# A batch's first scatter alone waits, earlier first loads and table fill, and three late jobs in a set order, in a two-layer cross-attention and mixture-of-experts kernel

## The chip, the cores and the metric

The kernel runs on one core of a Trainium2 chip. The metric is the time of one launch on the device in microseconds (us), as the median of several runs. Of the core's engines, PE (TensorE) multiplies matrices, and its weight loads are shown apart as PEld; DVE (VectorE) does element-wise work and reductions; ACT (ScalarE) does activations and copies; POOL (GpSimd) does some element-wise work and issues indirect DMAs; SP (SyncE) issues most of the loads. ACT and POOL issue DMAs of their own too.

## What is computed

`x` has 8 batches of 512 rows of 256 numbers; `ctx` has 64 rows of 256 for each batch. All is float32.

```
x = x + xattn0(layernorm(x), ctx)      # 16 heads of 16, softmax over 64 keys
x = x + ffn0(layernorm(x))             # per batch, the 384 rows with the highest router score
                                       # become gelu(row @ w_block), the others pass through
x = x + xattn1(layernorm(x), ctx, mask)
x = x + moe(layernorm(x))              # 8 experts, top 2 per row, softmax weights over the two
    moe: for each expert e: weight_e * (silu(row @ gate_e) * (row @ up_e)) @ down_e,  inner size 1024
```

## The kernel before

**Front part.** x lies in SBUF as 32 tiles of 128 rows. Each batch goes through one chain of 62 steps (L1183): attention of layer 0, the routed feed-forward, attention of layer 1, and the routing for the experts. A normalisation is `stats` (L373: batch statistics on DVE, then rstd by a power on POOL, L384), `scaled` (L387: a shift on DVE, then four ACT instructions, L393) and two `turned` steps (L401: transposes on PE into ps_x, copied by ACT). In the attentions `by_tokens` (L451) makes scores whose maxima DVE takes (L477), `by_keys` (L489) makes them again, turned, for ACT's exponentials (ex, L510), and `values`, `divided` and `added` finish. `biased` (L427) adds an output bias to x on POOL. Scores and exponentials share one PSUM buffer. Other chains are the constants ("s", `setups`, sorted by a number given to each), keys and values of the context ("k", "v"), ranks of the router ("A" to "H"), the lists of jobs ("l") and seven early expert jobs ("j").

The string `ORDER` (L49) says which chain takes its next step; 0 to 7 are the batches. `in_order` (L1209) ties each step's instructions on PE, DVE, ACT and POOL behind those of the steps ahead of it on the same engine, without a semaphore. So ORDER is the order of each engine's queue in the front part; loads on SP are not tied by it.

**First loads** (L157 to L192). SP starts with the context (ctxT, two halves), ACT with wk of layer 0, the four tiles of batch 0 and bk; POOL with wv, bv and bq of layer 0; SP goes on with wv and bv of layer 1, then wq, bo, wo of layer 0, batch 1 and all later things. vbd (L307) is a table that has to be filled with zeros once, half by DVE and half by POOL, before context values are put in; its fill has the number -0.85 among the constants, behind bq's scaling and ahead of headm.

**Scatter** (`sent_off`, L804). At the end of its chain each batch writes every row, with its number and weights, to two places in a DRAM buffer `xs` that is sorted by expert: two indirect DMAs from POOL for each of four row tiles, eight in all. They are declared free of each other, but the eighth takes a wait on the seven others, so that it can stand for all of them in what waits for the batch: the first early load waits for batch 3's last (L1083), and later batches follow it. Only the last batch's eight are waited for one by one.

**Late part.** 36 expert jobs of 256 rows ("full"), 128 rows ("one") or twice 64 rows ("pair"), in a fixed `order` (L1422): full, full, then pair, full, and one or full in turn. For each, `load` (L1251) reads expert and row numbers from the lists on SP and loads rows (xg) and 3 MB of weights, 6 MB for a pair; `enter` (L1305) turns the rows into xjT; `gate_up_full` or `gate_up_rows` multiplies by gate and up; `turn` (L1383) transposes the result of small jobs; `down` (L1391) multiplies by the down weights and adds the weighted rows to the output by an indirect DMA (L103). A pair's rows also wait for scatters of zero rows that pad the lists (L1029 to L1036). Only the first job's gates and the entries of the first two jobs are tied by `in_order`; for the rest of the late part the order on each engine is chosen when the program is built. The loop (L1437) enters the next job, then multiplies the job before it down.

Of the kernel before, what the change touches and what calls it, by code (L numbers as in the profile page):

```python
# [16 lines left out]
B = 8  # L17
# [7 lines left out]
TB = S // P  # L25
# [3 lines left out]
TOPK = 2  # L29
# [9 lines left out]
NLATE = NFULL - NEARLY  # L39
NONE = 7  # L40
NPAIR = 11
NJOB = NLATE + NONE + NPAIR
NUNIT = 2 * NPAIR
BIG = 65536.0
NG = H // 2
QR = 32
NQ = P // QR

ORDER = """  # L49
sssss0sss0ksk0s1020001s0k110s1vs0s031010s7s2s40v320v2410030v20120ss01040502A010A30A0As10  # L50
1013010343201130005s12010sk0112151761Bs2B1BB112120241201v102s2050223s022302412C22123C2C0
21C02131012110323150030sv02411033123104102523105200004331323426D14D34Ds14D2341v233613421
63233344212345412615434311432513431414312E25124E544E452356E54722434237252346535264345645
256352452F362F2325F63F464556355473355463574536743566474353567335566346v37l64763G464jj77j
5jGj666j5j7jj47Gjjj765j7457j4G5j64654j7j6556747j5j76446444j4746sH6jj56j557j76j7j57jj7Hsj
76jjjjHH7565j65jj676jj7jj6j57j5j6j75557j555jj57j6j667j7jjjs67j66j76j7676j66j76s667j676jj
jj7jjj77j7j7jjjjj77jjs7j7j7j7j7j77jj7jjjljj7jj7jj
"""


# [1 line left out]
def xattn_ffn_kernel(ctx: ExitStack, tc: tile.TileContext, a: dict, out: bass.AP):  # L62
    nc = tc.nc
# [25 lines left out]
    def after(i, others):  # L89
        for other in others:  # L90
            tc.add_manual_dep(
                i, other.name,
                mybir.DependencyInfo(mybir.DependencyClass.Sync, mybir.DependencyReason.DATA),
                reason="rows that it needs",
            )

    def apart(i, others, reason):
        for other in others:
            tc.declare_no_dep(i, other, reason=reason)
# [14 lines left out]
    with ExitStack() as front:  # L114
# [36 lines left out]
        def load_layer(l, names, q):  # L151
            for n in names:
                how = load_mat if n[0] == "w" else load_col if n in ("bk", "bq") else load_row
                layers[l][n] = how(q, f"{n}{l}")
# [6 lines left out]
            )  # L161
        load_layer(0, ("wk",), nc.scalar)
        for t in range(TB):
            nc.scalar.dma_start(x_sb[:, t, :], x_t[0][:, t, :])
        load_layer(0, ("bk",), nc.scalar)
        load_layer(0, ("wv", "bv", "bq"), nc.gpsimd)
        load_layer(1, ("wv", "bv"), nc.sync)
        load_layer(0, ("wq", "bo", "wo"), nc.sync)
        nc.sync.dma_start(x_sb[:, TB : 2 * TB, :], x_t[1])
        load_layer(1, ("wk", "bk"), nc.sync)  # L170
# [128 lines left out]
        turn = [0]  # L299
# [8 lines left out]
        for l in range(2):  # L308
            layers[l]["vbd"] = vbd[:, l]
        setups.append((  # L310
            -0.85, lambda: (nc.vector.memset(vbd[:, 0], 0.0), nc.gpsimd.memset(vbd[:, 1], 0.0)),
        ))

        def keys(l, c):
# [378 lines left out]
        def route_steps(b):  # L693
# [110 lines left out]
            def sent_off(t):  # L804
                slots, xr = got["slots"], got["xn"]

                sent = scattered.setdefault(b, [])
                for k in range(TOPK):  # L810
                    i = nc.gpsimd.indirect_dma_start(  # L811
                        out=xs,
                        out_offset=bass.IndirectOffsetOnAxis(ap=slots[:, t, k : k + 1], axis=0),
                        in_=xr[:, t, :],
                        in_offset=None,
                    ).ins
                    final = len(sent) == TB * TOPK - 1 and b < B - 1
                    if b >= B // 2:
                        apart(i, early_loads, "rows of other batches")
                    for other_i in sent:  # L820
                        if final:
                            tc.add_manual_dep(
                                i, other_i.name,
                                mybir.DependencyInfo(
                                    mybir.DependencyClass.Sync, mybir.DependencyReason.DATA
                                ),
                                reason="the last scatter stands for all",
                            )
                        else:
                            tc.declare_no_dep(i, other_i, reason="rows of their own")  # L830
                    sent.append(i)
                routed[:] = sent[-1:] if b < B - 1 else sent

            steps += [gates, logits, chosen, counted, weighed, placed]
            return steps + [lambda t=t: sent_off(t) for t in range(TB)]
# [227 lines left out]
        def early_steps(j):  # L1063
            got = {}

            def load():
                if not e_w:
                    e_w["gu"] = wpool[0].tile([P, NC, 2 * FF], F32, tag="wgu", name="e_wgu")
                    e_w["dn"] = wpool[0].tile([P, NF, D], F32, tag="wdn", name="e_wdn")
                with tc.issue_after(last.pop().ins) if last else nullcontext():  # L1070
                    row = nc.sync.value_load(
                        jobs_early[0:1, 0, j : j + 1], min_val=0, max_val=E * QROWS - P
                    )
                    e = nc.sync.value_load(jobs_early[0:1, 1, j : j + 1], min_val=0, max_val=E - 1)
                i = nc.sync.dma_start(
                    e_xg, xs[bass.ds(row, 2 * P), :].rearrange("(s p) w -> p s w", p=P)
                ).ins
                early_loads.append(i)

                for b in scattered:  # L1080
                    if b >= B // 2:
                        apart(i, scattered[b], "rows of other batches")
                after(i, scattered[B // 2 - 1][-1:])  # L1083
                got["e"] = e

            def load_piece(n):
# [122 lines left out]
        def in_order(step):  # L1209
            traced = nc.cur_bb.bb.instructions  # L1210
            last = traced[-1].name
            step()
            made = []
            for i in reversed(nc.cur_bb.bb.instructions):
                if i.name == last:
                    break
                made.append(i)
            for i in reversed(made):
                if i.engine not in engines:
                    continue  # L1220
                ahead = behind.setdefault(i.engine, [])
                for other in ahead:
                    tc.add_manual_dep(
                        i, other,
                        mybir.DependencyInfo(
                            mybir.DependencyClass.NoSync, mybir.DependencyReason.DATA
                        ),
                        reason="the order of the steps",
                    )

                if "DMA" not in type(i).__name__:
                    ahead.clear()
                ahead.append(i.name)
# [101 lines left out]
    def gate_up_full(j, xT, w):  # L1335
        wgu = w[0][0]
        hT = moe.tile([P, NF, 2 * P], F32, tag="hT", name=f"hT_{j}")
        for f in range(NF):
            ps = ps_gu.tile([P, 2, 2 * P], F32, tag="gu", name=f"gu_{j}_{f}")
            for half in range(2):  # L1340
                o = half * FF + f * P
                for c in range(NC):
                    nc.tensor.matmul(  # L1343
                        ps[:, half, :],
                        lhsT=wgu[:, c, o : o + P],
                        rhs=xT[:, c].rearrange("p s q -> p (s q)"),
                        start=(c == 0),
                        stop=(c == NC - 1),
                    )
            sg = moe.tile([P, 4 * P], F32, tag="sg", name=f"sg_{j}_{f}")  # L1350
            nc.scalar.activation(sg[:, 0 : 2 * P], ps[:, 0, :], AF.Silu)  # L1351
            nc.vector.tensor_tensor(hT[:, f, :], sg[:, 0 : 2 * P], ps[:, 1, :], ALU.mult)  # L1352
        return hT
# [78 lines left out]
    loads = [load_at(0), load_at(1)]  # L1432
    entered = []
    in_order(lambda: entered.append(enter(order[0], loads[0][0])))
    entered = entered[0]
    pending = None
    for i, j in enumerate(order):  # L1437
        xg, w = loads.pop(0)
        xT, tok, wt = entered
        if i > 0:  # L1440
            loads.append(load_at(i + 2))
        if i == 0:

            took_h = []
            in_order(lambda: took_h.append(gate_up_full(j, xT, w)))
            hT = took_h[0]
        elif j < NLATE:
            hT = gate_up_full(j, xT, w)
        else:
            h, hT = gate_up_rows(j, xT, w)  # L1450
        if i == 0:
            small_list()
            unit_list()
            loads.append(load_at(2))
        if i == 0:
            got_rows = []
            in_order(lambda: got_rows.append(enter(order[1], loads[0][0])))
            entered = got_rows[0]
        elif i + 1 < len(order):
            entered = enter(order[i + 1], loads[0][0])  # L1460
        if pending is not None:
            down(*pending)
        if j >= NLATE:
            turn(j, h, hT)
        pending = (j, hT, w, tok, wt)
    down(*pending)

# [44 lines left out]
```

## Time and profile before

| what | value |
|---|---|
| median of 3 runs | 1194.18 us (1190.78 to 1194.49) |
| the profiled execution | 1195.06 us |
| its span, first to last instruction | 1193.3 us |
| mean granted clock of PE | 0.993 |
| instructions | 21070 |
| DVE / ACT / POOL busy | 577.3 / 375.2 / 285.6 us |
| DMA moved | 209.96 MB, mean 176 GB/s |
| scatters to xs (L811) | 64, 975 ns each on POOL |
| indirect adds to the output (L103) | 65 late and 14 early ones |

In rows of the trace the first number is the start in us from the beginning of the span, the second the time in us; then come engine, line, operation, output<-input, shape, and how many instructions are put together. What stands in brackets is the engine's idle time just ahead of the row, and what ended it. The busy row of the page shows each fortieth of the span (29.8 us) as a digit, in tenths. Ends of matmuls are modelled, so a busy PE is not always at its peak. The front part reaches to about 587 us, the late part from there to the end.

### The profile page before, as it was taken

How to read it: one execution, taken by the hardware profiler on the slowest of the kernel's cores; microseconds unless marked ns; L12 is line 12 of the kernel's file. 1: busy time of each engine (PE TensorE's matmuls, PEld its weight loads, DVE VectorE, ACT ScalarE, POOL GpSimd, SP SyncE). 2: the span in 40 equal slices, each digit the busy share in tenths (PEclk: the TensorE clock that was granted, in tenths of full speed). 3: DMA queues.
4: the chain of work that ended last, by engine and by line, in shares of the span. 5: the costliest groups of instructions: out<-in, count | busy, mean ns of one | idle time of the engine just before them, and what ended most of it. 6: DMA issues, size and time to landing. Idle time of an engine off the chain costs nothing. (4 is left out here: it accounts for less than half of the span.)

```text
span 1193.3 us, 21070 instructions
## 1 busy us (share of the span) xinstructions
PE 1161.0 (97%) x8084; PEld 831.6 (70%) x8084; DVE 577.3 (48%) x1670; ACT 375.2 (31%) x718; POOL 285.6 (24%) x311
## 2 busy tenths in 40 slices
PE   6999999989999999999999999999999999999997
PEld 3655665655567778778877776876778767777676
DVE  6898787888787766655722121222222212222211
ACT  3655654644544342322211111211221112211211
POOL 5330223223330412322411212122121121121221
PEclk9999999999999999999999999999999999999999
DMA  9000001010025444445898689868897888967931
GB/s 265 2 1 2 1 19 38 23 51 33 24 80 170 123 127 131 114 146 151 276 340 285 216 284 307 305 209 313 294 310 256 278 302 308 311 227 270 313 112 18
DMA packets 122884, 209.96 MB, mean 176 GB/s; under 512 B 10912, under 2 KB 108064, under 8 KB 110752
## 3 DMA queue, kind: packets, MB, share of 16 engines
q1 hardware_dynamic: 102720, 185.64, 44.5%
q0 software_dynamic: 14848, 17.99, 7.5%
q10 hardware_dynamic: 5216, 4.98, 1.2%
q8 instruction: 64, 1.05, 0.4%
q14 instruction: 36, 0.29, 0.1%
HBM read 186.80 MB, written 23.73 MB: 176 GB/s over the span
## 5 line engine op out<-in xcount | busy, mean ns | idle before, releaser
L1343 PE MATMUL gu<-xjT,wgu 128*128 128x256 f32 x1152 | 253.8, 381 | 0.7 <-ACT xjT L1314 0.7
L1343 PEld LDWEIGHTS gu<-xjT,wgu 128*128 128x128 f32 x1152 | 218.7, 191 | 31.9 <-issue 1.5
L103 POOL DMA_INDIRECT out_dram<-now,tok x65 | 101.1, 1556 | 487.2 <-DVE now L1408 309.9
L1400 PE MATMUL o<-wdn,hT 128*128 128x256 f32 (+1 forms) x1040 | 193.0, 380 | 0.0
L1400 PEld LDWEIGHTS o<-wdn,hT 128*128 128x128 f32 (+1 forms) x1040 | 153.2, 172 | 29.5 <-issue 1.8
L1352 DVE TENSOR_TENSOR hT<-sg,gu 128x256 f32<-128x256 f32 x144 | 60.6, 421 | 192.9 <-ACT sg L1351 187.6
L1370 PE MATMUL gr<-wgu,xjT 128*64 128x512 f32 (+1 forms) x464 | 127.9, 596 | 0.0
L1351 ACT ACTIVATE sg<-gu 128x256 f32<-128x256 f32 x144 | 55.2, 383 | 204.8 <-PE gu L1343 200.7
L1132 PE MATMUL gu_e<-x_sb,e_wgu 128*128 128x256 f32 x448 | 103.2, 387 | 0.6 <-ACT x_sb L1111 0.6
L1132 PEld LDWEIGHTS gu_e<-x_sb,e_wgu 128*128 128x128 f32 x448 | 85.0, 192 | 15.9 <-issue 2.6
L1408 DVE TENSOR_SCALAR now<-o,wt 128x256 f32<-128x256 f32 x54 | 26.1, 484 | 144.2 <-PE o L1400 144.2
L1370 PEld LDWEIGHTS gr<-wgu,xjT 128*64 128x64 f32 (+1 forms) x464 | 45.0, 149 | 72.8 <-issue 71.0
L384 POOL TENSOR_TENSOR rstd<-ve,mhalf 128x4 f32<-128x4 f32 x32 | 32.8, 1026 | 233.8 <-DVE ve L382 180.7
L811 POOL DMA_INDIRECT xs<-xr,slots x64 | 62.4, 975 | 104.5 <-issue 57.6
L477 DVE TENSOR_REDUCE mx<-sc 128x32 f32<-128x2048 f32 x32 | 73.2, 2288 | 22.2 <-PE sc L470 19.0
L1380 DVE TENSOR_TENSOR h<-sg,gr 128x512 f32<-128x512 f32 x36 | 24.7, 687 | 87.3 <-PE gr L1370 87.3
L440 PE MATMUL ps_q<-xT,w_wq 128*128 128x512 f32 x128 | 63.5, 625 | 0.5 <-ACT xT L411 0.5
L1379 ACT ACTIVATE sg<-gr 128x512 f32<-128x512 f32 x36 | 21.5, 597 | 135.1 <-PE gr L1370 135.1
L571 PE MATMUL py<-w_wo,cT 128*128 128x256 f32 x256 | 60.3, 384 | 0.0
L393 ACT ACTIVATE xn<-x_sb,shift,rstd 128x256 f32<-128x256 f32 x96 | 49.8, 593 | 19.6 <-DVE shift L390 18.3
L571 PEld LDWEIGHTS py<-w_wo,cT 128*128 128x128 f32 x256 | 47.3, 190 | 11.6 <-issue 5.3
L379 DVE BATCH_NORM_STATS2 st<-x_sb 128x6 f32<-128x256 f32 x128 | 51.4, 401 | 6.6 <-DMA x_sb<-in_x_dram 6.4
(288 smaller groups left out, 1457.0 us busy)
## 6 DMA issues: line engine op xcount, KB each, us to landing
wgu<-in_guT_dram SPq DMA_DIRECT2D x94, 1024.0 KB
wdn<-in_dnT_dram SPq DMA_DIRECT2D x47, 1024.0 KB
e_wgu<-in_guT_dram SPq DMA_DIRECT2D x56, 256.0 KB
e_wdn<-in_dnT_dram SPq DMA_DIRECT2D x7, 1024.0 KB
xg<-xs SPq DMA_DIRECT2D x18, 260.0 KB
out_dram<-x_sb ACTq DMA_DIRECT2D x8, 512.0 KB
x_sb<-in_x_dram SPq DMA_DIRECT2D x7, 512.0 KB
x_sb<-xs SPq DMA_DIRECT2D x7, 260.0 KB
```

What stands on the lines that cost most here:

```text
L103: i = nc.gpsimd.indirect_dma_start(out=out_rows, out_offset=bass.IndirectOffsetOnAxis(ap=tok, axis=0), in_=rows, in_offset=None, bounds_ch ...
L379: nc.vector.bn_stats(st, x_sb[:, b * TB + t, :])
L440: nc.tensor.matmul(ps, lhsT=w["wq"][:, k, c * P : (c + 1) * P], rhs=got["xT"][:, k, :], start=(k == 0), stop=(k == NC - 1),)
L477: nc.vector.tensor_reduce(got["mx"].rearrange("p t (r h) -> p r t h", r=NQ)[:, :, :, 2 * c : 2 * c + 2], sc, AX.X, ALU.max,)
L571: nc.tensor.matmul(py[:, s, :], lhsT=cT[:, c, t * P : (t + 1) * P], rhs=w["wo"][:, c, :], start=(c == 0), stop=(c == NC - 1),)
L811: i = nc.gpsimd.indirect_dma_start(out=xs, out_offset=bass.IndirectOffsetOnAxis(ap=slots[:, t, k : k + 1], axis=0), in_=xr[:, t, :], in_of ...
L1132: nc.tensor.matmul(ps[:, half, :], lhsT=e_w["gu"][:, c, o : o + P], rhs=e_xT[:, c].rearrange("p s q -> p (s q)"), start=(c == 0), stop=(c ...
L1343: nc.tensor.matmul(ps[:, half, :], lhsT=wgu[:, c, o : o + P], rhs=xT[:, c].rearrange("p s q -> p (s q)"), start=(c == 0), stop=(c == NC - 1),)
L1351: nc.scalar.activation(sg[:, 0 : 2 * P], ps[:, 0, :], AF.Silu)
L1352: nc.vector.tensor_tensor(hT[:, f, :], sg[:, 0 : 2 * P], ps[:, 1, :], ALU.mult)
L1370: nc.tensor.matmul(ps[rows], lhsT=xT[:, c, 0, rows], rhs=wgu[:, c, o : o + 4 * P], start=(c == 0), stop=(c == NC - 1),)
L1400: nc.tensor.matmul(ps[rows], lhsT=hT[:, f, s * P + rows.start : s * P + rows.stop], rhs=wdn[:, f, :], start=(f == 0), stop=(f == NF - 1),)
```

## The change

- ORDER is written anew, with the same steps.
- The fill of vbd gets the number -0.93 and so comes first of all constants, on DVE and on POOL.
- Of batch 0's four tiles two are now issued by ACT and two by SP; wv and bq of layer 0 go from POOL to ACT, behind the tiles; wv of layer 1 comes behind SP's tiles; bv of both layers goes to POOL.
- In a batch's scatter the first waits for the eight of the batch ahead; the other seven are declared free of both batches' scatters. The eighth waits for nothing more, and whatever waited for it waits for all eight.
- The first three jobs of the late part are put through `in_order` in all their steps: entry, gates, the down product of the job ahead, and turn.

```diff
+NPIN = 3
...
 ORDER = """
-sssss0sss0ksk0s1020001s0k110s1vs0s031010s7s2s40v320v2410030v20120ss01040502A010A30A0As10
...
+ssssss0ss0ksk0120000102sk0s11v25001ss0s3400310s2v14ss10s030s20sv172004010A00102A03A01A01
...
         for t in range(TB):
-            nc.scalar.dma_start(x_sb[:, t, :], x_t[0][:, t, :])
-        load_layer(0, ("bk",), nc.scalar)
-        load_layer(0, ("wv", "bv", "bq"), nc.gpsimd)
-        load_layer(1, ("wv", "bv"), nc.sync)
+            q = (nc.scalar, nc.scalar, nc.sync, nc.sync)[t]
+            q.dma_start(x_sb[:, t, :], x_t[0][:, t, :])
+        load_layer(0, ("bk", "wv", "bq"), nc.scalar)
+        load_layer(1, ("wv",), nc.sync)
+        load_layer(0, ("bv",), nc.gpsimd)
+        load_layer(1, ("bv",), nc.gpsimd)
         load_layer(0, ("wq", "bo", "wo"), nc.sync)
...
         setups.append((
-            -0.85, lambda: (nc.vector.memset(vbd[:, 0], 0.0), nc.gpsimd.memset(vbd[:, 1], 0.0)),
+            -0.93, lambda: (nc.vector.memset(vbd[:, 0], 0.0), nc.gpsimd.memset(vbd[:, 1], 0.0)),
         ))
...
-                    final = len(sent) == TB * TOPK - 1 and b < B - 1
                     if b >= B // 2:
                         apart(i, early_loads, "rows of other batches")
-                    for other_i in sent:
-                        if final:
-                            tc.add_manual_dep(
...
-                        else:
-                            tc.declare_no_dep(i, other_i, reason="rows of their own")
+                    if sent:
+                        apart(i, sent + scattered.get(b - 1, []), "rows of their own")
+                    elif b > 0:
+                        after(i, scattered[b - 1])
                     sent.append(i)
-                routed[:] = sent[-1:] if b < B - 1 else sent
+                routed[:] = sent
...
-                after(i, scattered[B // 2 - 1][-1:])
+                after(i, scattered[B // 2 - 1])
...
+    def placed(i, step):
+
+        if i < NPIN:
+            got = []
+            in_order(lambda: got.append(step()))
+            return got[0]
+        return step()
...
     for i, j in enumerate(order):
...
-        if i == 0:
-
-            took_h = []
-            in_order(lambda: took_h.append(gate_up_full(j, xT, w)))
-            hT = took_h[0]
-        elif j < NLATE:
-            hT = gate_up_full(j, xT, w)
+        if j < NLATE:
+            hT = placed(i, lambda: gate_up_full(j, xT, w))
         else:
-            h, hT = gate_up_rows(j, xT, w)
+            h, hT = placed(i, lambda: gate_up_rows(j, xT, w))
...
-        elif i + 1 < len(order):
-            entered = enter(order[i + 1], loads[0][0])
+        if i + 1 < len(order):
+            entered.append(placed(i, lambda: enter(order[i + 1], loads[0][0])))
         if pending is not None:
-            down(*pending)
+            placed(i, lambda: down(*pending))
         if j >= NLATE:
-            turn(j, h, hT)
+            placed(i, lambda: turn(j, h, hT))
```

More of the change, by code (lines that the diff above doesn't have):

```diff
@@ L49 @@
 ORDER = """
-sssss0sss0ksk0s1020001s0k110s1vs0s031010s7s2s40v320v2410030v20120ss01040502A010A30A0As10
[L51 to L57, printed above, removed]
+ssssss0ss0ksk0120000102sk0s11v25001ss0s3400310s2v14ss10s030s20sv172004010A00102A03A01A01
+010310342015v21031030010v021s1v612k511BB2125B021071251B102120201243042s0123202C102032C12
+13122C6C10s12132v10301203502104s331231s14220032102040303130113D4D746D324461D24v323133143
+2632135345341623461245324114241315114E2s541E4E2534E3244324455372724542323255345236344564
+2556354254F32F22655F42353F663546756355345456646357s473455653765336436373l336457j6jj47467
+5jj746G6j5j4j4jGj4j5j7jj6G7jGj67s6j765j5sj45j74j5j67jj5j47j7465754s76j6j7467446H4567j675
+j7H6jH5Hj56j565jjjj67j7jj766j7j5jj5577j56jj75jjj655j6756j6j77j6sj676j7667j6j6677jj667j66
+7jjj7jj7jj77jjjjj77js7jj77jjj77j77jjj7j7jlj7jjjjj
 """
@@ L816, in sent_off @@
                     ).ins
-                    final = len(sent) == TB * TOPK - 1 and b < B - 1
                     if b >= B // 2:
                         apart(i, early_loads, "rows of other batches")
-                    for other_i in sent:
-                        if final:
-                            tc.add_manual_dep(
[L823 to L828, printed above, removed]
-                        else:
-                            tc.declare_no_dep(i, other_i, reason="rows of their own")
+                    if sent:
+                        apart(i, sent + scattered.get(b - 1, []), "rows of their own")
+                    elif b > 0:
+                        after(i, scattered[b - 1])
                     sent.append(i)
-                routed[:] = sent[-1:] if b < B - 1 else sent
+                routed[:] = sent
             steps += [gates, logits, chosen, counted, weighed, placed]
@@ L1434, in xattn_ffn_kernel @@
     in_order(lambda: entered.append(enter(order[0], loads[0][0])))
-    entered = entered[0]
+    def placed(i, step):
[4 more added lines that the diff above has]
+        return step()
     pending = None
     for i, j in enumerate(order):
-        xg, w = loads.pop(0)
-        xT, tok, wt = entered
+        w = loads.pop(0)[1]
+        xT, tok, wt = entered.pop(0)
         if i > 0:
             loads.append(load_at(i + 2))
-        if i == 0:
-            took_h = []
-            in_order(lambda: took_h.append(gate_up_full(j, xT, w)))
-            hT = took_h[0]
-        elif j < NLATE:
-            hT = gate_up_full(j, xT, w)
+        if j < NLATE:
+            hT = placed(i, lambda: gate_up_full(j, xT, w))
         else:
-            h, hT = gate_up_rows(j, xT, w)
+            h, hT = placed(i, lambda: gate_up_rows(j, xT, w))
         if i == 0:
@@ L1454, in xattn_ffn_kernel @@
             loads.append(load_at(2))
[L1455 to L1458, printed above, removed]
-        elif i + 1 < len(order):
-            entered = enter(order[i + 1], loads[0][0])
+        if i + 1 < len(order):
+            entered.append(placed(i, lambda: enter(order[i + 1], loads[0][0])))
         if pending is not None:
-            down(*pending)
+            placed(i, lambda: down(*pending))
         if j >= NLATE:
-            turn(j, h, hT)
+            placed(i, lambda: turn(j, h, hT))
         pending = (j, hT, w, tok, wt)
```

## The prediction

> **What bounds the kernel now.** I read the page's first two parts, then who kept TensorE (PE) waiting, then stretches, then rows in order of time at the start, around the scatters and at the first late jobs.
>
> ```profile
> PE 1161.0 (97%) x8084; PEld 831.6 (70%) x8084; DVE 577.3 (48%) x1670; ACT 375.2 (31%) x718; POOL 285.6 (24%) x311
> PE   6999999989999999999999999999999999999997
> ```
>
> PE is busy in 1161.0 of 1193.3 us. The change takes no matmul away, so it can win only from the 32.3 us in which PE stands, and from time that PE runs slowly. By 25 us stretches the 32.3 divide thus: 9.1 in the first 25 us, 7.4 behind the last matmul (it ends at 1186.04), 15.8 between 25 and 625 us, and nothing from 625 us to the last matmul. The waits of PE:
>
> ```profile
> PE ps_k L318 <- DMA pre<-in_wk_dram: 5.1, 1, 5.1
> PE st L493 <- ACT ex L510: 4.5, 3, 2.5
> PE ps_x L408 <- ACT xn L393: 3.7, 2, 3.5
> PE ps_x L1312 <- DMA xg<-xs: 2.5, 2, 2.3
> ```
>
> Each line gives total us, times, longest. The third line is the start, the second the scatters of batches 0 and 1, the fourth the first late jobs. PE also pays behind some gaps. In the next view the columns are the stretch, its length, busy time of PE, PEld, DVE, ACT and POOL, then PE's granted clock, DMA share and GB/s:
>
> ```profile
> 5.00:11.00 6.00, 5.74 (x8) 2.24 (x8) 2.56 (x10) 1.29 (x2) 0.70 (x5) 1.00 1.11 293
> 16.00:20.00 4.00, 3.76 (x7) 1.70 (x6) 3.68 (x15) 0.88 (x3) 1.48 (x3) 0.57 1.07 328
> 193.00:197.00 4.00, 3.84 (x20) 1.25 (x24) 3.76 (x14) 0.94 (x3) 3.90 (x7) 0.57 0.09 33
> 521.00:525.00 4.00, 4.00 (x12) 3.24 (x12) 2.85 (x7) 1.00 (x3) 0.96 (x1) 0.57 0.67 198
> 605.00:609.00 4.00, 3.62 (x13) 2.99 (x14) 0.65 (x5) 0.37 (x1) 0.00 (x0) 0.70 0.88 344
> ```
>
> At clock 0.57 a stretch of 4 us loses 4 x 0.43 = 1.7 us. There are four such places: after the start, in the scatters of batch 0 and of batch 6, and at the late jobs (4 x 0.30, and 4 x 0.12 in the next 4 us, 1.7 again). A gap that triggers this costs its length plus 1.7.
>
> **Start: loads and table fill.** Rows of PE, DVE and POOL:
>
> ```profile
> 9.53 0.43 DVE L379 BATCH_NORM_STATS2 st<-x_sb 128x6 f32<-128x256 f32 x1 [0.70 <-DMA x_sb<-in_x_dram]
> 10.99 1.04 POOL L384 TENSOR_TENSOR rstd<-ve,mhalf 128x4 f32<-128x4 f32 x1 [3.76 <-DVE ve L382]
> 11.34 1.76 DVE L311 MEMSET vbd<- 128x2048 f32 x1 [0.37 <-issue]
> 13.05 0.14 DVE L390 SCALAR_TENSOR_TENSOR shift<-mv,rstd 128x4 f32<-128x4 f32 x1
> 14.37 0.83 PE L408 MATMUL ps_x<-ident,xn 128*128 128x128 f32 x3 [3.52 <-ACT xn L393]
> ```
>
> PE finishes the keys at 5.11 + 5.74 = 10.85 and waits until 14.37 for batch 0's normalised rows. They are late twice. rstd is done at 12.03, but shift stands behind the 1.76 us fill of vbd on DVE: 13.05 - 12.03 = 1.0 us. And the third and fourth 128-row tiles of x, issued by 3.6 us, land only about 9.5 and 9.9 us, because wv of both layers (256 KB each) moves among them. The change moves the fill to the front, where DVE has nothing until 6.15 us, and the two wv behind the four x tiles. A rule stands against the other half of the edit, two x tiles issued from SP in place of ACT: the Trainium skill, "DMA: Bandwidth & Descriptors", section "Issuing engines are not separate DMA queues", says that all issuers' transfers interleave on the same 16 engines and a second issuer saves issue time only. By it the second issuer is worth the last ACT issues, under 1 us; I count it zero, and count bytes alone: 512 KB ahead less, at the 293 GB/s of the row above, 1.75 us. So shift comes at 13.05 - 1.0 - 1.75 = 10.3, ps_x 1.3 later (as now, 14.37 - 13.05) at 11.6, and the gap falls from 3.5 to 0.8: -2.75. I let the slow stretch at 16 to 20 go with it (-1.7), since a gap of 1.04 at 297 us was followed by none.
>
> Against that: counted from the two order strings with this trace's step times, the first 25 us of PE work carry 28 us of DVE work in the new order and 23 in the old (statistics of batches 2, 4 and 5 come sooner). DVE was busy 15.45 of the first 25 us, so most fits; I charge 0.5. The statistics of batch 2 now stand ahead of batch 0's first maximum on DVE; if those rows are late, that maximum and PE wait us for us. On POOL the other half of the fill (1.79) goes ahead of mhalf, which stood at 3.41 and will stand near 4.5; rstd needs it near 9. ACT's warm-up follows it, with 3 us to spare before xn. bq0 now comes behind wv0 on ACT's queue, and its scaling stands ahead of shift on DVE: zero if it lands by 10 us (its scaling ran at 10.82 without a wait), otherwise us for us. Sum of the start: -4.0, bounds 0 and -5.5.
>
> **Scatters.** Every batch sends eight scatters; now the eighth waits until the seven before it have landed:
>
> ```profile
> 187.50 0.96 POOL L811 DMA_INDIRECT xs<-xr,slots  x1 [0.30 <-issue]
> 188.77 0.96 POOL L811 DMA_INDIRECT xs<-xr,slots  x1 [0.31 <-DMA xs<-xr,slots]
> 192.12 0.96 POOL L811 DMA_INDIRECT xs<-xr,slots  x1 [2.38 <-issue]
> 193.16 1.75 PE L493 MATMUL st<-qT,kbd 32*128 32x512 f32 x8 [2.48 <-ACT ex L510]
> ```
>
> The wait is 2.38 instead of 0.31: 2.07 us in each of batches 0 to 6, 14.5 us of POOL. Behind it on POOL stand the bias add (L430) and rstd (L384), and behind those the next normalisation; but all that waited for rstd in the whole trace is DVE's shift, 3.1 us. So as a queue it is worth little. What the trace shows beyond that is odd: in the bursts matmuls are answered late. The scores' last matmul (L501) ends at 188.76, and ACT's ex starts at 191.17; elsewhere (251.04 to 251.16) this takes 0.12. PE then has nothing until 193.16. Over the seven bursts with the wait, each about 12 us long, PE stands 2.4, 2.4, 2.2, 0.95, 0, 0 and 0.9 us: 8.9 of the 15.8. Without the wait a burst is 2.07 of about 12 us shorter. Bounds: 0 if the late answers come from the scatters themselves, and -8.9 - 3.4 (two slow stretches) if the wait makes them. I take -2.5, nearer to the first, because late answers also stand ahead of the wait (L571 ends at 186.84, its add starts at 188.91).
>
> The added wait: a batch's first scatter waits for the eight of the batch ahead. The nearest row has batch 0's last at 192.12 and batch 1's first at 236.69: 40 us of cover, so zero; behind it would stand seven scatters, the bias add and rstd. The first early load (L1075) and the lists wait for eight instead of one, and the last of the eight goes out 2 us sooner; PE has no idle from 350 to 500 us, so zero.
>
> **Three late jobs in order.** PE took the entry of the third job in order (a pair, whose rows wait for the padding scatters) ahead of the second job's gate matmuls:
>
> ```profile
> 602.27 1.22 SPq L1272 DMA_DIRECT2D xg<-xs  x2
> 605.38 0.41 PE L1312 MATMUL ps_x<-ident,xg 128*128 128x128 f32 x2 [2.28 <-DMA xg<-xs]
> 605.63 1.03 PE L1400 MATMUL o<-wdn,hT 128*128 128x256 f32 x4
> 606.49 15.66 PE L1343 MATMUL gu<-xjT,wgu 128*128 128x256 f32 x64
> ```
>
> Pinned, the gates of the second job in order run first: they need only xjT, copied at 603.14 for 0.58 us, so PE waits about 0.7 (603.10 to 603.75) where it waited 2.28: -1.6. A rule weighs here: the Trainium skill, "TensorE: Matmul & The Clock Gate", Part 1, has the clock fall after an idle window of about 3.4 us. By it a gap of 2.28 should not cost a slow phase, and the pin is worth 1.6. The row shows the slow phase all the same (15.66 us for 64 matmuls; the next such set at 643.42 takes 13.98). I follow the row: -1.6 - 1.7 = -3.3, bounds -1.6 and -4. The cover is the second job's weights: issued at 587.18 (2 x 1 MB) and behind 3 MB of the first job's, at 317 GB/s they are there by 600. The third job's 4 MB, issued by 605.9, take 12 us at 330 GB/s: 618, and PE comes to them near 625.
>
> **Sum.** -4.0 - 2.5 - 3.3 = -9.8. The rest of the new order I count at zero: the same steps, the same PE and DVE work up to every later 25 us mark within 4 us, and the full PE row behind 25 us passes the start's gain on. Against the profiled execution (1195.06 us, of which the span is 1193.3) this is 1185.3; that execution is 0.9 above the median of the runs, so I say 1184.5.
>
> **Rivals.** (a) As summed: 1184.5, own range 1180 to 1189; chance 0.50. (b) The start's gain is eaten by DVE or a late load and the bursts stay: only the pin, -3.3, 1191; chance 0.26. For it: both DMA and DVE are dense in the first 25 us, and late answers exist without the wait. (c) The wait makes the late answers: -4.0 - 3.3 - 8.9, less what DVE needs anyway, about -15: 1179; chance 0.12. (d) Slower: the new order puts PE work that needs an answer into the bursts. Place: the bursts of batches 3 to 6, which pay 0.95, 0, 0 and 0.9 + 1.7 now, 3.6 in all. Price: a burst paid in full is 2.4 idle + 1.7 slow = 4.1. Start and pin give 7.3, so it decides from about two more full bursts; all four would be +16.4 less 3.6, less 7.3: +5.5, 1200. For it: three of seven bursts already pay 2.2 or more; against: from 400 us on, early jobs' matmuls stand between. Chance 0.12. That the change does nothing on one of its three counts is in (b).
>
> (a), (c) and half of (b) are faster by over 0.3% (about what a measurement of this kernel can tell from no change): 0.75; the other half within it: 0.13; (d): 0.12. The range leaves out (d) and the far half of (c): 1177 to 1195.
>
> **What would show it.** Right: shift near 10.3 and no 0.57 stretch at 16 to 20; all eight scatters 0.3 apart; gates of the second late job straight after its xjT, 64 matmuls in 14 us. Wrong: a DVE wait on x_sb in the first 25 us; PE idle in bursts still near 8.9 or above (the -2.5 is then lost); a new gap between 25 and 575 us.

## The result and the profile after

The changed kernel took 1208.72 us in the median of 4 runs (1207.66 to 1211.07), the kernel before, beside it, 1194.03 us (4 runs, 1190.78 to 1194.49): ratio 1.0123, 95% interval 1.0097 to 1.0149. It is 1.2% slower, where 1184.5 was forecast. The profiled execution took 1209.29 us, its span is 1207.6 us, 14.3 more than before. The busy time of PE and its tenths by slice, from the page of the changed kernel:

```profile
PE 1167.7 (97%) x8084; PEld 832.9 (69%) x8084; DVE 578.3 (48%) x1670; ACT 376.0 (31%) x718; POOL 285.5 (24%) x310
PE   7999998999989999989999999999999999999997
```

The same 8084 matmuls are busy 6.7 us longer, so PE ran slowly more often, and it also stood longer. Who kept it waiting (total us, times, longest; in the front part line numbers are 3 higher than before):

```profile
PE st L496 <- ACT ex L513: 4.8, 1, 4.8
PE sc L464 <- ACT ex L513: 3.4, 2, 2.4
PE pz L540 <- issue: 2.9, 4, 1.1
PE st L496 <- DVE mx L480: 2.0, 1, 2.0
...
PE py L574 <- DVE cT L563: 1.9, 1, 1.9
PE ps_x L411 <- ACT xn L396: 1.8, 4, 1.3
PE gu L1338 <- ACT xjT L1309: 1.4, 2, 0.7
```

The start (ps_x, 3.7 before) and the late jobs (2.5 before, now 1.4 of another wait) have shrunk. What grew lies in the front part: waits for ACT and DVE, and waits for which the profile shows no releaser ("issue"). Stretches of the changed kernel, columns as in the prediction; the first is the slow stretch of the start, now at full clock, the next five lie in and just behind scatters of batches 0, 1, 2, 3 and 6:

```profile
16.00:20.00 4.00, 4.00 (x39) 2.04 (x38) 3.69 (x18) 1.37 (x2) 1.02 (x1) 1.00 1.07 323
193.00:197.00 4.00, 1.40 (x8) 0.87 (x12) 3.86 (x11) 2.92 (x4) 4.00 (x6) 0.64 0.00 0
252.00:260.00 8.00, 5.85 (x88) 3.51 (x92) 6.39 (x15) 4.56 (x7) 2.61 (x4) 0.79 0.00 0
304.00:312.00 8.00, 5.93 (x57) 2.28 (x57) 7.59 (x22) 2.52 (x4) 1.04 (x1) 0.79 0.01 2
356.00:364.00 8.00, 5.30 (x58) 3.42 (x61) 0.00 (x0) 2.93 (x4) 4.43 (x7) 0.62 0.55 158
536.00:544.00 8.00, 6.10 (x20) 4.75 (x20) 4.26 (x8) 1.23 (x4) 0.00 (x0) 0.79 0.41 128
```

Up to the last matmul such phases lose 11.9 us of clock (the shortfall from full clock, summed over 4 us stretches), against 6.8 before.

Now the span divides into three parts: up to the 200th matmul, from there to the first scatter of batch 7, and the rest. Before they are 38.6, 525.1 and 629.6 us; after, 35.4, 545.8 and 626.4. So -3.2, +20.7 and -3.2: the start and the late jobs gave most of what was forecast for them, and the middle, where the scatters are, took three times as much. The middle itself, by view of stretches, before and after, with 4877 matmuls each:

```profile
38.63:563.74 525.11, 513.09 (x4877) 352.61 (x4870) 397.59 (x1113) 242.88 (x432) 143.86 (x186) 0.99 0.23 70
```

```profile
35.38:581.22 545.84, 523.47 (x4877) 355.75 (x4870) 398.81 (x1111) 241.65 (x428) 148.20 (x192) 0.98 0.22 67
```

PE idles 22.4 us in it (545.84 - 523.47) where it idled 12.0, and is busy 10.4 longer at the lower clock. The scatters themselves did what was said. Rows of POOL, PE and ACT in the burst of batch 0, changed kernel:

```profile
181.97 1.14 POOL L814 DMA_INDIRECT xs<-xr,slots  x1 [9.76 <-ACT xT L414]
...
187.46 1.04 PE L504 MATMUL st<-mxT,minus 32*128 32x512 f32 x8
...
189.79 0.96 POOL L814 DMA_INDIRECT xs<-xr,slots  x1 [0.31 <-issue]
191.06 0.98 POOL L814 DMA_INDIRECT xs<-xr,slots  x1 [0.30 <-issue]
...
193.61 1.94 ACT L513 ACTIVATE ex<-st 128x1024 f32<-128x1024 f32 x2 [3.84 <-remote]
...
195.60 2.09 PE L496 MATMUL st<-qT,kbd 32*128 32x512 f32 x8 [4.79 <-ACT ex L513]
```

All eight go out 0.30 apart. The scores are done at 188.50 (187.46 + 1.04), and ACT, idle for 3.84 us, starts on them at 193.61: 11.6 us after the first scatter. In the kernel before this happened 10.2 us after the first scatter (191.17, scatter at 180.95), inside the 2.38 us for which the eighth waited. When the scatters' data stop moving is read from DMA (last two columns) in the changed kernel:

```profile
192.50:193.00 0.50, 0.00 (x0) 0.00 (x0) 0.50 (x1) 0.00 (x0) 0.50 (x1) 1.00 0.73 266
193.00:193.50 0.50, 0.00 (x0) 0.00 (x0) 0.50 (x3) 0.00 (x0) 0.50 (x2) 1.00 0.01 0
```

So ACT starts some 0.5 us after the last data of the burst.

### The profile page after: what moved, and what is told of

Same layout as the page of the kernel before. It is cut to its first block, busy times and chain, and to the rows that moved or that the text cites. A ratio compares the mean times of both kernels' runs of the same rounds, so it can differ in the third digit from the quotient of the medians.

```text
span 1207.6 us, 21071 instructions
## 1 busy us (share of the span) xinstructions
PE 1167.7 (97%) x8084; PEld 832.9 (69%) x8084; DVE 578.3 (48%) x1670; ACT 376.0 (31%) x718; POOL 285.5 (24%) x310
## 4 chain that ended last, share of the span: by engine, by line
PE 64%; issue 13%; DMA 12%; DVE 4%; ACT 2%; POOL 2%; another core or an unknown queue 1%; POOLq 0%; ACTq 0%; SPq 0%; DVEq 0%
DMA out_dram<-now,tok 11%; PE gu L1338 10%; PE gu_e L1127 8%; PE o L1395 7%; PE gr L1365 5%; PE py L574 4%; PE o_e L1154 4%; PE ps_q L443 4%; PE st L496 3%; PE ctx L525 2%; PE sc L473 2%; PE st L504 2%; PE ps_x L411 2%; PE pz L540 2%; PE pf L658 2%
## 5 line engine op out<-in xcount | busy, mean ns | idle before, releaser
L574 PE MATMUL py<-w_wo,cT 128*128 128x256 f32 x256 | 63.2, 393 | 2.7 <-DVE cT L563 1.9
L574 PEld LDWEIGHTS py<-w_wo,cT 128*128 128x128 f32 x256 | 47.8, 193 | 14.3 <-issue 4.8
```

What stands on the lines that cost most here:

```text
L574: nc.tensor.matmul(py[:, s, :], lhsT=cT[:, c, t * P : (t + 1) * P], rhs=w["wo"][:, c, :], start=(c == 0), stop=(c == NC - 1),)
```

## The experiments

Theory one after this view: in a burst of scatters the answers of matmuls (the semaphore that tells ACT and DVE that PE is done) are held, and the eighth's wait was the break that let them through; without it they are held to the last landing. Theory two: the wait doesn't matter, the new order puts work badly into the bursts.

Each run below is measured beside the kernel before on the same chip. The chips are of two kinds, which shows only here: on chips 3, 4, 12 and 14 the kernel before takes 1179.7 to 1182.1 us, on chips 2 and 15 1195.3 to 1196.1, as in the record (1194.0). I call them quick and late chips; ratios are compared within a kind.

### One part undone or done alone (chip 3, quick)

a1_wait_back is the changed kernel with before's scatter rule:

```diff
-                    if sent:
-                        apart(i, sent + scattered.get(b - 1, []), "rows of their own")
-                    elif b > 0:
-                        after(i, scattered[b - 1])
+                    final = len(sent) == TB * TOPK - 1 and b < B - 1
+                    for other_i in sent:
+                        if final:
+                            tc.add_manual_dep(
...
+                        else:
+                            tc.declare_no_dep(i, other_i, reason="rows of their own")
...
-                routed[:] = sent
+                routed[:] = sent[-1:] if b < B - 1 else sent
...
-                after(i, scattered[B // 2 - 1])
+                after(i, scattered[B // 2 - 1][-1:])
```

> The changed kernel with the old scatter rule put back: the eighth scatter of each batch waits for the seven before it. All else, the new order too, as changed. Theory one (in a burst of scatters matmul answers are held until the last of them has landed; the eighth's wait was the break that let them through): the PE gaps in the bursts fall from about 18 us back to about 9, the clock drops that follow the long gaps go, and the time comes to 1184 to 1190 us. Theory two (the new order places matmuls that need an answer, and DVE work, badly in the bursts; the wait doesn't matter): within 3 us of the changed kernel, 1206 to 1211.

b1_rule is the kernel before with the opposite edit and nothing else.

> The kernel before with nothing but the new scatter rule (first scatter of a batch waits for the batch ahead, no wait at the eighth). Old order, loads, fill and late jobs. Theory one: PE gaps in the bursts grow from 8.9 us to 15 or more, and the time to 1203 to 1213 us, since the answers come after the last landing. Theory two: the old order was sound in the bursts, so it loses nothing and may save the 2 us a burst that the eighth waits on POOL: 1190 to 1195.

b2_start_pin is the kernel before with the diff's loads, the number -0.93, NPIN and `placed`; ORDER only has its "s" of the fill moved to the front:

```diff
-sssss0sss0ksk0s1020001s0k110s1vs0s031010s7s2s40v320v2410030v20120ss01040502A010A30A0As10
+ssssss0ss0ksk0s1020001s0k110s1vs0s031010s7s2s40v320v2410030v20120ss01040502A010A30A0As10
```

> The kernel before with the new first loads, the table fill as the first setup step (the rest of the order as before) and the three late jobs in set order; the scatter rule of before. Both theories: the start gives 3 us and the pins 3 us, 1186 to 1190 us. If instead the loads or the pins cost something that the changed kernel's trace hides: 1193 or above.

b3_order is the kernel before with the diff's ORDER and the number -0.93.

> The kernel before with the new order of steps and the fill's place in it, nothing else; old scatter rule, loads and late jobs. Theory one: the order alone costs little, 1190 to 1197 us, with PE gaps in the bursts at 7 to 11 us. Theory two: the order carries the loss, 1205 to 1215 us.

Measured: a1_wait_back 1182.94 us, 1.0031 (1.0014 to 1.0049); b1_rule 1178.73, 0.9984 (0.9973 to 0.9995); b2_start_pin 1175.24, 0.9957 (0.9938 to 0.9976); b3_order 1184.94, 1.0041 (1.0031 to 1.0051). No part alone costs 1.2%, and the missing wait alone loses nothing (it gains 0.2%, hardly clear of none): both theories fail as they stood. But in these four traces no matmul's semaphore update came more than 0.08 us after its end, so there were no late answers for theory one to act on. In each of the two traces of the record 37 came over 0.3 us late by the records, though some of that is lost records (916 updates of 926 before, 907 of 919 after; here none is missing).

### The changed kernel on other chips (chips 12 and 4, quick)

c1_after and d1_after are the changed kernel as it is; c0_before the kernel before; c2_order_rule is b3_order with b1_rule's edit; c3_start_pin_rule is b2_start_pin with b1_rule's edit, that is, the changed kernel with the old order; d2_wait_back is a1_wait_back again.

> The changed kernel as it is, beside the kernel before on one chip. In the trace of the record a matmul's answer (its semaphore update) in a burst of scatters came 2 to 9 us after its end; in the four experiments so far none came later than 0.05 us, and the kernel before took 1179.7 there and not 1194.0. Theory one (the held answers make the loss, and they are a state of the chip or of the execution that is not always there): with answers at 0.05 us the change costs what its order costs and gains what loads, pins and rule gain, 1176 to 1184 us, ratio 0.998 to 1.004; if answers are held again, ratio 1.010 to 1.015. Theory two (the new order and the missing wait make the loss together, whatever the chip): ratio 1.010 to 1.015 with answers at 0.05 us too.

> The kernel before with the new order and the new scatter rule, old loads and late jobs. Theory one with quick answers: the order's 1.0041 by the rule's 0.9984, about 1.0025, 1181 to 1185 us where before is 1179.7. Theory two: 1.012 to 1.018, since the start and the pins that help are left out.

> The kernel before with the new loads, the fill first, the pinned late jobs and the new scatter rule; the old order. Where answers are quick: 0.9957 by 0.9984, ratio 0.993 to 0.996, 1172 to 1175 us where before is 1179.7, below both kernels. Where they are held: above before, 1.003 to 1.010.

> The kernel before, as it is, for its profile on the chip of these runs. Theory one: the matmul answers in the bursts come within 0.05 us, PE has no gap above 1 us in bursts 0 to 3, and the span is near 1178; if the span is near 1193 the answers are held by 2 us and more again.

> The changed kernel again, to see whether this run has late matmul answers. Both traces of the record have them, and lost records beside them; the eight experiments have none, and there the change gave 0.9946. If answers are late by 2 us and more in the bursts: ratio 1.010 to 1.015. If they come within 0.05 us: 0.992 to 0.997. A ratio above 1.008 without late answers would say that the late answers are not the cause.

> The changed kernel with the eighth's wait put back, on the same chip. If answers are late: theory one (the missing wait takes away the break that let them through) 0.995 to 1.003; theory two (the order is at fault) 1.008 to 1.015. If answers are quick: 1.0031 as before, 0.8% above the changed kernel, since the new order was laid out with no wait in mind and the wait then delays what is behind it.

Measured: c1_after 1176.02 us, 0.9946 (0.9928 to 0.9964), and d1_after 1176.53, 0.9954 (0.9940 to 0.9969): here the change is faster by half a per cent. c2_order_rule 1180.13, 0.9981 (0.9965 to 0.9997); c3_start_pin_rule 1175.92, 0.9948 (0.9927 to 0.9969); c0_before 1185.74 in one run, span 1184.0; d2_wait_back 1181.33, 0.9992 (0.9976 to 1.0007), 0.4% above the changed kernel on the same chip. The burst of batch 0 in c1_after, rows of PE, ACT and POOL:

```profile
187.53 1.04 PE L504 MATMUL st<-mxT,minus 32*128 32x512 f32 x8
...
188.64 1.94 ACT L513 ACTIVATE ex<-st 128x1024 f32<-128x1024 f32 x2 [1.32 <-PE st L504]
...
190.82 1.14 PE L496 MATMUL st<-qT,kbd 32*128 32x512 f32 x8
...
191.12 0.99 POOL L814 DMA_INDIRECT xs<-xr,slots  x1 [0.30 <-issue]
```

It is the same program with the same scatters at the same times, 0.06 to 0.08 us later than in the record. The scores end at 188.57, ACT starts at 188.64, and PE goes on at 190.82 without a gap; on the record's chip ACT started at 193.61. So neither the order nor the missing wait makes PE stand here: the late answer does, and it goes with the chip, not with the program (chips 3 and 12, met more than once, were quick each time). The middle part on quick chips, before (c0_before), changed (c1_after), changed with the old order (c3_start_pin_rule), and old order with the eighth's wait (b2_start_pin):

```profile
38.32:553.32 515.00, 509.36 (x4877) 351.14 (x4870) 399.21 (x1113) 243.22 (x432) 144.68 (x186) 1.00 0.23 71
```

```profile
35.46:548.19 512.73, 510.05 (x4877) 351.06 (x4870) 399.00 (x1111) 241.76 (x428) 148.11 (x193) 1.00 0.24 71
```

```profile
36.34:547.30 510.96, 507.69 (x4877) 350.32 (x4870) 399.50 (x1113) 243.20 (x432) 144.15 (x187) 1.00 0.23 72
```

```profile
35.78:546.76 510.98, 507.71 (x4877) 350.71 (x4870) 399.06 (x1113) 243.18 (x432) 144.70 (x186) 1.00 0.23 72
```

c0_before is no fair measure: its execution is 4.2 us above the median of the same kernel on its chip (1181.52), and in its middle PE waits 2.4 us for the rows of an early job (up to 346.55), which b2_start_pin doesn't have. In the old order the middle is 511.0 us with the eighth's wait (b2_start_pin, and 511.1 in h2_start_pin below) and without it (c3_start_pin_rule, and b1_rule), so on a quick chip dropping the wait is worth nothing there, and not the 2.5 forecast. The new order is 2 us longer without the wait (512.7, and 513.1 in d1_after) and 7 to 8 longer with it (517.8 in a1_wait_back, 518.7 in d2_wait_back). What the change gains on quick chips is the start and the late jobs.

### More packets in the bursts (chip 2, late)

```diff
+    spray = dram.tile([4, 64, P], F32, name="spray")
...
                 sent = scattered.setdefault(b, [])
+                if t == 0 and b < 4:
+                    with nc.allow_non_contiguous_dma(reason="small packets"):
+                        nc.sync.dma_start(spray[b].rearrange("w p -> p w"), xr[:, 1, 0:64])
```

> The kernel before with 8192 packets of 4 bytes added in each of the first four bursts (64 columns of the rows, written to a scratch in DRAM through SP's queue as the burst begins; the output doesn't depend on it). It asks whether crowded DMA engines are what makes matmul answers late in the record. If so: answers 2 us and more late while the packets move, PE gaps of 2 us and more in bursts 0 to 3, and the time 8 to 15 us above the kernel before. If the late answers have another cause: answers within 0.05 us, and the time within 3 us of the kernel before.

> The changed kernel with the same packets in the same four bursts. If crowded DMA engines make answers late: above e1_before_traffic by 0.5% or more where the missing wait or the order exposes it. If not: 1175 to 1180 us, about 0.5% below the kernel before, as without the packets.

Measured: e1_before_traffic 1218.38 us, 1.0176 (1.0147 to 1.0206) of before (1196.10); e2_after_traffic 1240.78, 1.0368 (1.0330 to 1.0406). The packets didn't keep to the bursts: each set takes some 25 us or more, and the first moves from about 153 to 183 us, before batch 0's scatters at 192.5. So they show something else: answers come late outside the bursts too. In e1_before_traffic, a stretch between the scatters of batches 1 and 2, and its rows of PE and ACT:

```profile
276.00:280.00 4.00, 3.73 (x29) 2.19 (x21) 3.86 (x13) 0.69 (x2) 0.00 (x0) 1.00 1.35 1
```

```profile
276.27 1.04 PE L502 MATMUL st<-mxT,minus 32*128 32x512 f32 x8
...
279.57 2.12 ACT L511 ACTIVATE ex<-st,maskc 128x1024 f32<-128x1024 f32 x2 [3.11 <-PE ps_l L722]
...
281.75 0.75 PE L494 MATMUL st<-qT,kbd 32*128 32x512 f32 x4 [2.01 <-ACT ex L511]
```

The scores end at 277.31 and ACT starts on them at 279.57, 2.26 us later, while the packets keep the DMA engines busy and move 1 GB/s: it is packets and not bytes that go with the late answer. (In the record's trace of before no answer is over 0.3 us late between 247 and 293 us, between the same two bursts.) Both kernels lose to the packets, 22 us before (1218.38 - 1196.10) and 32 us changed (1240.78 - 1208.72, the record). Not all of it is late answers: the longest single gap of e1_before_traffic, 9.54 us up to 179.73, stands within a group of score matmuls and is ended by nothing that the profile shows, and from 155 to 170 PE kept on without a gap beside the packets. Nor does it show that a quick chip would stand the same packets without loss; these two ran on a late one only.

### The wait put back, and the old order, on a late chip

The same kernels on further chips: f1_wait_back and g1_wait_back are a1_wait_back; f2_old_order, h1_old_order and i1_old_order are c3_start_pin_rule; h2_start_pin is b2_start_pin.

> The changed kernel with the eighth's wait put back, in the hope of a chip where answers are late (there the kernel before takes about 1195 us, elsewhere about 1180). On such a chip: theory one (the wait's break lets the answers through) 0.994 to 1.003 of before; theory two (the order is at fault) 1.007 to 1.014. On a chip with quick answers: 0.998 to 1.004, and nothing is told apart.

> The changed kernel with the old order of steps (the fill still first), no wait at the eighth. On a chip with late answers: theory one 1.003 to 1.012 of before, since the answers are held to the last landing whatever the order; theory two 0.990 to 0.997. On a chip with quick answers: 0.993 to 0.996 as before.

> The changed kernel with the eighth's wait put back, once more in the hope of a chip with late answers (the kernel before then takes about 1195 us). There: theory one (the missing wait) 0.994 to 1.003 of before, theory two (the order) 1.007 to 1.014. With quick answers: 0.998 to 1.004, nothing told apart.

> The changed kernel with the old order of steps (fill first), no wait at the eighth, in the hope of a chip with late answers. There, where g1_wait_back fell from 1.012 to 1.0018: theory one (the missing wait alone, whatever the order) 1.003 to 1.012 of before; theory two (the wait is missed only by the new order) 0.990 to 0.998. With quick answers: 0.993 to 0.996, nothing told apart.

> The kernel before with the new loads, the fill first and the pinned late jobs, the old order and the eighth's wait. Start and pins touch no burst, so both theories say the same on either kind of chip: 0.992 to 0.997 of before, which would make it the one version below before on both kinds.

> The changed kernel with the old order, no wait at the eighth, once more. With late answers (before near 1195): theory one (the missing wait whatever the order) 1.003 to 1.012, theory two (the wait is missed only by the new order) 0.990 to 0.998. With quick answers 0.993 to 0.996, nothing told apart.

Five of the six met quick chips, where the two theories say the same: f1_wait_back 1181.43 us, 0.9997 (0.9982 to 1.0011); f2_old_order 1174.94, 0.9954 (0.9939 to 0.9968); h1_old_order 1175.38, 0.9952 (0.9933 to 0.9970); h2_start_pin 1174.84, 0.9947 (0.9931 to 0.9963); i1_old_order 1174.83, 0.9937 (0.9918 to 0.9956). g1_wait_back met a late one, chip 15: 1196.53 us beside 1195.28, ratio 1.0018 (1.0001 to 1.0035), against 1.0123 for the changed kernel. The same burst in g1_wait_back, rows of PE, ACT and POOL:

```profile
187.76 1.14 PE L504 MATMUL st<-mxT,minus 32*128 32x512 f32 x8
...
189.92 0.96 POOL L814 DMA_INDIRECT xs<-xr,slots  x1 [0.30 <-DMA xs<-xr,slots]
192.34 1.94 ACT L513 ACTIVATE ex<-st 128x1024 f32<-128x1024 f32 x2 [3.86 <-PE pf L658]
192.69 1.26 POOL L814 DMA_INDIRECT xs<-xr,slots  x1 [1.81 <-DMA xs<-xr,slots]
...
194.33 1.91 PE L496 MATMUL st<-qT,kbd 32*128 32x512 f32 x8 [3.11 <-ACT ex L513]
```

The data of the seven stop before 192.0:

```profile
191.50:192.00 0.50, 0.00 (x0) 0.00 (x0) 0.47 (x3) 0.00 (x0) 0.00 (x0) 1.00 0.59 208
192.00:192.50 0.50, 0.00 (x0) 0.00 (x0) 0.46 (x3) 0.16 (x1) 0.00 (x0) 1.00 0.00 0
```

The answers come while the eighth stands: ACT starts at 192.34, 10.25 us after the first scatter, and the eighth goes out at 192.69. PE's gap is 3.11 us where it was 4.79. Batch 3 is alike: ACT's ex starts at 348.65 with the eighth going out at 349.00, and in the changed kernel at 358.16 with the eighth out at 355.56. The whole middle:

```profile
35.48:567.27 531.79, 515.59 (x4877) 352.98 (x4870) 398.54 (x1111) 242.19 (x428) 147.92 (x192) 0.99 0.23 69
```

It is 14.0 us shorter than in the changed kernel (545.8), 6.2 of it idle time of PE (22.4 to 16.2) and 7.9 of it busy time at a better clock; the lost clock falls from 11.9 to 3.4 us. By the two ratios it is worth 12.5 us (1.0123 - 1.0018, of 1194). So on a late chip, under the new order, the missing wait costs 12 to 14 us, and theory two, by which the wait doesn't matter, fails. Whether the old order would miss it as much is not shown. The new order with the wait still has a middle 6.7 us longer than the kernel before (525.1), much as on quick chips (518.7 in d2_wait_back, 511.0 in b2_start_pin): the order costs too, the lesser part.

## Why the prediction was wrong

- **Start**, predicted -4.0: -3.2 measured (200th matmul at 38.63 before, 35.38 after). The slow stretch at 16 to 20 is gone, and shift follows rstd without the fill, both as predicted. The loads were over-sized: DVE's ve, behind the last statistics, came at 10.11 and not 10.74, 0.6 sooner where 1.75 was counted by bytes. So shift came at 11.44, not 10.3, and ps_x's gap is 1.32, not 0.8. bq0's scaling did wait for its load, 0.69, but rstd set the time of shift. Rows of DVE, POOL and PE of the changed kernel:

```profile
10.11 0.17 DVE L385 TENSOR_SCALAR ve<-mv 128x4 f32<-128x4 f32 x1
10.36 1.05 POOL L387 TENSOR_TENSOR rstd<-ve,mhalf 128x4 f32<-128x4 f32 x1 [1.64 <-DVE ve L385]
10.97 0.17 DVE L294 TENSOR_SCALAR c_bq<-c_bq 128x2 f32<-128x2 f32 x1 [0.69 <-DMA c_bq<-in_bq_dram]
...
11.44 0.17 DVE L393 SCALAR_TENSOR_TENSOR shift<-mv,rstd 128x4 f32<-128x4 f32 x1 [0.24 <-POOL rstd L387]
...
12.39 0.73 PE L411 MATMUL ps_x<-ident,xn 128*128 128x128 f32 x2 [1.32 <-ACT xn L396]
```

- **Pins**, predicted -3.3: -3.2 measured behind batch 7's first scatter. The gates follow xjT with a gap of 0.68, as predicted 0.7, and 64 of them take 14.08 us, as predicted 14:

```profile
621.34 14.08 PE L1338 MATMUL gu<-xjT,wgu 128*128 128x256 f32 x64 [0.68 <-ACT xjT L1309]
```

- **Scatters**, predicted -2.5: this step failed, and its sign with it. It measured +14.0 on a late chip. "Bounds: 0 if the late answers come from the scatters themselves, and -8.9 - 3.4 (two slow stretches) if the wait makes them" leaves out the third case, that the wait is what ends them. The late answers come with the scatters on this kind of chip, and the last of them are let go when the seven have landed and nothing follows. The change took that moment away, so they are held for one scatter more: +14.0 us of the middle by g1_wait_back, more than half of it clock lost behind the longer gaps. The trace of before held the hint: ex at 191.17 starts inside the eighth's wait, 189.74 to 192.12. The add at 188.91 starts ahead of it, so not every answer is held that long. The prediction saw that add ("late answers also stand ahead of the wait") and the late ex, and didn't ask what releases them.
- **The rest of the new order**, counted at zero: this step failed too, by less. It costs 6.7 us on a late chip with the wait in place; on quick ones 2 without it and 7 to 8 with it. Rival (d) saw a loss in the bursts, and put it on the order in batches 3 to 6; the slow stretches lie in batches 0, 1, 2, 3 and 6, and the order carries the lesser part. Rival (c), by which the wait makes the late answers, has the sign reversed.
- **Added wait**, zero: no run shows a cost; in the changed kernel the scatters of a batch start 29.7 us and more behind the last of the batch ahead.

So -3.2 - 3.2 + 14.0 + 6.7 = +14.3, the difference of the spans. That the parts add up proves nothing: the middle's 20.7 is split by one trace, g1_wait_back, from a late chip that need not be the record's. On four quick chips, where answers aren't late, the change or its old-order twin takes 0.994 to 0.995 of before. The prediction's sign holds there, by its start and its pins and not by its scatters.

What stays open: what makes a chip late or quick; and what the old order without the wait costs on a late chip, since all four runs of it met quick ones. A rival is untested: that the recording of the profile has a part in it. The traces of late chips lack records (16 of 919 updates of PE in g1_wait_back), those of quick ones next to none, and no run here tells whether the recording holds the answers. On quick chips the changed kernel (0.9946 and 0.9954) and the start and pins in the old order, with or without the wait (0.9947 to 0.9957 and 0.9937 to 0.9954), can't be told apart by these runs; on a late chip the old-order ones were not run.

## What to carry to other kernels

When a trace shows something unusual beside a wait, here late answers in a burst of scatters, look at what releases it before pricing the wait's removal: the release fell inside the wait, so the bound on the other side of zero belonged in the sum. A wait that costs POOL 2 us was worth 2 us a burst to PE on a late chip (14 us over seven bursts), and nothing on a quick one in the old order. And a gain of half a per cent that rests on how soon engines answer each other should be measured on more than one chip.

## What the runs showed of the hardware

- One program takes 1180 us on four chips and 1195 on two others, with the scatters' pace alike (0.30 us apart). In bursts of indirect scatters matmul answers come within 0.1 us on the first (188.57 to 188.64 in c1_after), and up to some 5 us late on the others (188.50 to 193.61 in the record). That this is the whole of the 15 us isn't shown.
- On a late chip the last held answers of a burst come a fraction of a microsecond after the scatters' data stop: data to about 193.1 and ACT at 193.61 in the record, to about 192.0 and 192.34 in g1_wait_back.
- A gap of PE shorter than 3 us can lower the clock or not: in b1_rule a gap of 2.0 us at the first late jobs was followed by no slow phase there, in c2_order_rule one of 2.3 us was (clock 0.57 from 592 to 596 us). In the changed kernel one of 1.9 us at 538.47 was too, in g1_wait_back one of 1.7 at 526.20 not. This is why, as far as these traces tell, the pins are worth 1.1 us beside b1_rule (627.1 us behind batch 7's first scatter, 626.0 in c3_start_pin_rule) and 3.2 in the record.
